# A GRU on one core: five filling units ahead of the first turn of h, none behind the second

## The chip, the cores and the metric

The kernel runs on one NeuronCore of a Trainium2 chip. The metric is the device time of a whole launch in microseconds; the times shown before are three runs of the kernel, and one further execution was profiled.

## The reference

A gated recurrent unit walks over 128 time steps, with 64 batch rows, an input of 512 and a hidden state of 512; its states are added to the input. Everything is float32. Cut to what is computed:

```python
def step(h, inp):
    x_t, prop = inp                      # prop: every fourth step but the last
    comb = jnp.concatenate([x_t, h], axis=-1)
    z = jax.nn.sigmoid(comb @ Wz + bz)
    r = jax.nn.sigmoid(comb @ Wr + br)
    comb2 = jnp.concatenate([x_t, r * h], axis=-1)
    h_cand = jnp.tanh(comb2 @ Wh + bh)
    h_new = (1.0 - z) * h + z * h_cand
    h_next = jnp.where(prop, jnp.tanh(h_new @ Wp + bp), h_new)
    return (h_next, h_new)
out = x + ys                             # ys: h_new of every step
```

Each weight has 1024 rows: the upper 512 act on x_t, the lower 512 on h (or r * h).

## The kernel before

**Layout.** The state of 64 x 512 is held as 128 partitions x 256: the upper 64 partitions have the first half of the hidden units, the lower 64 the second half. A product of the state with 512 x 512 weights needs the state transposed, since the state is the stationary operand of the matmul. `turn` (L195) does this: four bf16 transposes on TensorE move one half of the state (128 columns) into the PSUM tile `turn`, and one copy (L193, by the engine named in the call) brings it into SBUF. The transposed state is `hT`, the transposed r * h is `rhT`; each has two halves, c = 0 and c = 1. `product` (L186) multiplies one quarter of the rows of a weight; a full product of state and weight is four of them, in an order in which the first two need only half c = 0 of the transposed state (16 matmul records in all, 1.91 us).

**A step** (loop over t, 128 times) is written in this order, and each engine runs its instructions in the order of the program (the schedule is written by hand; a framework adds the semaphores):

1. the R product of hT (L576), then `read_out` and, on ScalarE and VectorE, the sigmoid and r * h (L598, L599);
2. the Z product of hT, the turns of r * h into rhT, sigmoids of z (L613, L614) and `keep` = (1 - z) * h (L615); then `fill(places[0])`;
3. the candidate's product of rhT (L624);
4. for each half of 128 columns: tanh on ScalarE (L637), times z on VectorE (L638), plus keep on VectorE (L643), which gives that half of `h_new`;
5. filling units, the turn of the first half of h, copied by VectorE; one unit; the turn of the second half, copied by ScalarE; filling units (L646 to L653);
6. in every fourth step ("prop") a further product with Wp, a tanh and turns of that result;
7. work for later on GpSimd (sums of input products), the addition of h_new to x, DMAs of x in and of results out on SyncE's queue.

The PSUM regions `rc` and `zp` hold the three gates' sums; ScalarE writes the input's part of the next step's gates into them (`seed`, L384), and the recurrent products add to that.

**Filling units.** The products of x with the upper halves of the weights don't depend on h. They are cut into small units that stand in a list (`queue`), and `fill(n)` (L390) puts the next n of them into TensorE's stream at that place. `PLACES` says how many units a step takes in its two or three places:

```python
PLACES = (
    (6, 8, 6), (2, 6), (6, 6), (2, 6), (6, 8, 6), (2, 6), (2, 6), (6, 8),
)
```

The entry is chosen by (t - 3) mod 8. The first number goes ahead of the candidate's product, the second behind it, the third (prop steps) around the turn that follows Wp. From t = 3 on the units are those of `batch` (L427): the inputs of eight steps are multiplied by two levels of a Strassen-like scheme, with 49 products instead of 64; a unit is one such block product, four matmul records of 192 columns, and 14 units make a batch. When the eighth and the fourteenth unit of a batch have been placed, an "end" (copies on ScalarE, additions on VectorE, L450 to L460, which read the PSUM tiles scratch_q, r, a, x) waits in `pending` until the next `read_out`. The first three steps take 12 units in either place, plain products of 256 columns. The units of the last group are used up in t = 122; later steps have none.

Of the kernel before, what the change touches and what calls it, by code (L numbers as in the profile page):

```python
# [17 lines left out]
def kernel(  # L18
# [176 lines left out]
    def turn(src, dst, c, name, eng):  # L195


        pt = turn_ps[c][:, :P].bitcast(BF16).rearrange("p (w n) -> p w n", w=2)
        for s in range(S):
            words = src[:, c * P + s * B : c * P + (s + 1) * B].bitcast(BF16)  # L200
            for w in range(2):
                nc.tensor.transpose(  # L202
                    pt[s * B : (s + 1) * B, w, :],
                    words.rearrange("p (n w) -> p w n", w=2)[:, w, :],
                    ident16,
                )
        copy(
            eng,
            dst[:, c, :].bitcast(U16).rearrange("p (n w) -> p n w", w=2),
            pt.bitcast(U16).rearrange("p w n -> p n w"),  # L210
        )
# [178 lines left out]
    def fill(n):  # L390
        for _ in range(min(n, len(queue))):
            unit, end = queue.pop(0)
            unit()
            if end is not None:
                pending.append(end)

    def read_out():
        while pending:
            pending.pop(0)()
# [157 lines left out]
    for t in range(T):  # L557
# [6 lines left out]
        places = PLACES[u]  # L564
        if t < 3:
            queue.extend(plain(2 * t + 2) + plain(2 * t + 3))
            places = (12, 12)
        elif t == 3:
            queue.extend(batches(FIRST))
            places = (8, 8, 6)  # L570
# [72 lines left out]
            nc.vector.tensor_add(h_new[:, ts(c, P)], pc, keep[:, ts(c, P)])  # L643
        seed(H_, t + 1)
        read_out()
        fill(places[1] - 3 if places[1] > 6 else 4)  # L646
        h = h_new
        if not last:
            hT = new_T("hT", f"hT_{t}")
            turn(h, hT, 0, f"hT_{t}", nc.vector)  # L650
            fill(1)
            turn(h, hT, 1, f"hT_{t}", nc.scalar)
        fill(2 if places[1] > 6 else 1)  # L653
        if t == 2:
            sum_outer_1()
        if t == 3:
# [131 lines left out]
```

## Time and profile before

| what | value |
|---|---|
| median of three runs | 1371.43 us (1371.06 to 1373.5) |
| the profiled execution | 1370.75 us |
| its span, first to last instruction | 1368.9 us |
| mean granted TensorE clock | 0.998 |
| TensorE matmuls, weight loads | 15336 each |
| DMA traffic | 73.86 MB, mean 54 GB/s |

How to read it: PE is TensorE's matmuls, PEld its weight loads, which run ahead of and beside the matmuls; DVE is VectorE, ACT ScalarE, POOL GpSimd, SPq SyncE's queue of DMA issues. A timeline line gives start and duration in us, engine, line of the program, operation, what is written and read, the shape, how many instructions were merged into the line, and in brackets the idle time before it with what ended it. Matmul records overlap each other, as their ends are modelled. `L177` is the line of every matmul of a product or unit, `L202` of every transpose, `L193` of every copy behind a turn; their tiles tell them apart.

### The profile page before, as it was taken

What the parts mean: (1) busy time and instruction counts of PE and PEld (TensorE: products, weight loads), DVE (VectorE), ACT (ScalarE), POOL (GpSimd) and SP (SyncE); (2) the same over time, 40 slices, a digit from 0 to 9 for tenths busy, and PEclk for the clock granted to TensorE, in tenths of its full rate; (3) what the DMA queues carried; (4) which work ended last, traced back from release to release, by engine and by line L of the source; (5) the groups of instructions that cost most, each with busy time, mean ns of one, the idle gap of its engine ahead of it and who ended that gap; (6) DMA issues with size and microseconds to landing.
All of it is one profiled execution on the core that took longest, in us unless ns stands there. A gap on an engine that the chain in (4) does not pass through costs nothing.

```text
span 1368.9 us, 37448 instructions
## 1 busy us (share of the span) xinstructions
PE 1342.6 (98%) x15336; PEld 1028.9 (75%) x15336; DVE 689.2 (50%) x1875; ACT 631.2 (46%) x1857; POOL 938.7 (69%) x1139
## 2 busy tenths in 40 slices
PE   7999999999999999999999999999999999999996
PEld 4777777777777777777777777777777777777764
DVE  4245554555555555554555555555555555555543
ACT  1234445445444445445445444445445445454443
POOL 4327676787767786677686767786677686767740
PEclk9999999999999999999999999999999999999999
DMA  9002212212231222212222131222212222131010
GB/s 286 11 17 48 63 32 63 63 33 63 49 77 32 60 36 63 63 32 63 52 43 63 43 83 34 49 46 63 63 32 63 48 48 63 35 76 33 17 33 16
DMA packets 113572, 73.86 MB, mean 54 GB/s; under 512 B 61556, under 2 KB 109812, under 8 KB 113400
## 3 DMA queue, kind: packets, MB, share of 16 engines
q1 hardware_dynamic: 112336, 69.68, 22.5%
q8 instruction: 121, 1.98, 0.6%
q10 hardware_dynamic: 1064, 1.78, 0.4%
q14 instruction: 51, 0.42, 0.1%
HBM read 39.99 MB, written 16.78 MB: 41 GB/s over the span
## 4 chain that ended last, share of the span: by engine, by line
PE 96%; DMA 2%; DVE 1%; ACT 0%; issue 0%; SPq 0%; DVEq 0%; ACTq 0%
PE rc L177 33%; PE zp L177 20%; PE scratch_q L177 11%; PE scratch_x L177 10%; PE scratch_r L177 10%; PE turn L202 6%; PE scratch_a L177 6%; DMA early<-in_x_dram 1%; DMA wx<-in_L_cond_Wz_dram 1%; DMA wh<-in_L_cond_Wr_dram 1%; DVE h L643 0%; DVE turn L638 0%; ACT xT L193 0%; SPq L93 0%; DVE tw L300 0%
## 5 line engine op out<-in xcount | busy, mean ns | idle before, releaser
L177 PE MATMUL rc<-wh,rhT 128*64 128x256 f32 x2048 | 246.6, 381 | 2.0 <-ACT zp L614 2.0
L485 POOL TENSOR_TENSOR cp<-mb,mb 128x768 f32<-128x768 f32 x75 | 136.6, 1821 | 112.1 <-ACT rc L384 67.1
L177 PEld LDWEIGHTS rc<-wh,rhT 128*64 128x64 f32 x2048 | 158.9, 137 | 55.0 <-ACT zp L614 12.4
L177 PE MATMUL rc<-wh,hT 128*64 128x256 f32 x1536 | 183.1, 380 | 0.5 <-DVE hT L193 0.2
L177 PE MATMUL zp<-wh,hT 128*64 128x256 f32 x1536 | 183.2, 379 | 0.0
L722 POOL TENSOR_TENSOR xr<-xr,h 128x256 f32<-128x256 f32 x127 | 92.5, 729 | 102.1 <-DVE h L643 95.5
L193 DVE COPY rhT<-turn 128x256 uint16<-128x256 uint16 x256 | 96.8, 420 | 127.1 <-PE turn L202 127.1
L638 DVE TENSOR_TENSOR turn<-turn,z 128x128 f32<-128x128 f32 x256 | 75.5, 295 | 161.0 <-ACT turn L637 161.0
L485 POOL TENSOR_TENSOR cp<-mb 128x768 f32<-128x768 f32 x45 | 81.9, 1820 | 108.4 <-ACT rc L384 107.2
L177 PEld LDWEIGHTS zp<-wh,hT 128*64 128x64 f32 x1536 | 117.5, 137 | 47.4
L177 PEld LDWEIGHTS rc<-wh,hT 128*64 128x64 f32 x1536 | 111.6, 137 | 45.2 <-issue 1.0
L598 ACT ACTIVATE turn<-rc 128x128 f32<-128x128 f32 x256 | 55.4, 260 | 156.6 <-issue 85.6
L452 DVE TENSOR_TENSOR cx<-scratch_r,cx 128x384 f32<-128x384 f32 x105 | 58.6, 558 | 128.7 <-ACT cx L450 128.7
L193 ACT COPY hT<-turn 128x256 uint16<-128x256 uint16 x127 | 47.3, 373 | 155.8 <-PE turn L202 96.6
L485 POOL TENSOR_TENSOR mb<-mb,mb 128x768 f32<-128x768 f32 x60 | 109.2, 1820 | 13.4 <-DVE mb L460 13.4
L458 DVE TENSOR_TENSOR mb<-scratch_r,cq 128x384 f32<-128x384 f32 x105 | 58.6, 558 | 88.1 <-ACT cq L457 88.1
L384 ACT COPY rc<-cp 128x256 f32<-128x256 f32 x254 | 95.8, 377 | 11.6 <-POOL s L325 0.4
L637 ACT ACTIVATE turn<-rc 128x128 f32<-128x128 f32 x256 | 57.0, 262 | 90.3 <-PE rc L177 90.3
L613 ACT ACTIVATE z<-zp 128x256 f32<-128x256 f32 x128 | 49.2, 384 | 104.0 <-PE zp L177 104.0
L202 PEld LDWEIGHTS <-h 128*64 128x64 bf16 x1016 | 47.4, 109 | 51.0 <-DVE h L643 46.0
L384 ACT COPY zp<-cp 128x256 f32<-128x256 f32 x127 | 47.9, 377 | 78.1 <-DVE keep L615 78.1
L202 PE MATMUL turn<-ident,h 128*64 128x128 bf16 x1016 | 76.6, 227 | 5.4 <-DVE h L643 5.4
(149 smaller groups left out, 2954.6 us busy)
## 6 DMA issues: line engine op xcount, KB each, us to landing
xr<-in_x_dram SPq DMA_DIRECT2D x62, 256.0 KB, 4.2
out_dram<-xr SPq DMA_DIRECT2D x62, 256.0 KB, 3.3
xs<-in_x_dram SPq DMA_DIRECT2D x56, 256.0 KB, 4.3
wh<-in_L_cond_Wr_dram SPq DMA_DIRECT2D x2, 512.0 KB, 7.6
wh<-in_L_cond_Wz_dram SPq DMA_DIRECT2D x2, 512.0 KB, 8.3
wh<-in_L_cond_Wh_dram SPq DMA_DIRECT2D x2, 512.0 KB, 10.4
early<-in_x_dram SPq DMA_DIRECT2D x4, 256.0 KB, 13.1
wp<-in_L_cond_Wp_dram SPq DMA_DIRECT2D x1, 1024.0 KB
```

The lines of the kernel that those rows point to most:

```text
L177: nc.tensor.matmul(ps[s * B : (s + 1) * B], lhsT=lhs, rhs=rhs(s), start=start, stop=True, skip_group_check=True,)
L193: (eng.copy if eng is nc.scalar else eng.tensor_copy)(dst, src)
L202: nc.tensor.transpose(pt[s * B : (s + 1) * B, w, :], words.rearrange("p (n w) -> p w n", w=2)[:, w, :], ident16,)
L384: nc.scalar.copy(cut(slots[i]), G[t][:, :, i, :])
L452: nc.vector.tensor_add(T2[n], r_ps, T2[n])
L458: nc.vector.tensor_add(blocks()[:, :, 0, 1], r_ps, q2)
L485: nc.gpsimd.tensor_add(dst, a, b)
L598: nc.scalar.activation(act_ps[c], slots[R][:, ts(c, P)], AF.Sigmoid)
L613: nc.scalar.activation(z, slots[Z], AF.Sigmoid)
L637: nc.scalar.activation(pc, slots[H_][:, ts(c, P)], AF.Tanh)
L638: nc.vector.tensor_mul(pc, pc, z[:, ts(c, P)])
L722: nc.gpsimd.tensor_add(xr[g][:, j, :], xr[g][:, j, :], h_new)
```

## The change

Only the second place of a step is cut otherwise. Before: with more than six units, three fewer than all lie ahead of the first turn of h, one between the turns, two behind; with six units four, one and one. After: five ahead, one between, and the rest behind. So steps of eight units keep 5, 1, 2; steps of six go from 4, 1, 1 to 5, 1, 0; the first three steps (twelve units) go from 9, 1, 2 to 5, 1, 6.

```diff
         seed(H_, t + 1)
         read_out()
-        fill(places[1] - 3 if places[1] > 6 else 4)
+        fill(5)
         h = h_new
         if not last:
             hT = new_T("hT", f"hT_{t}")
             turn(h, hT, 0, f"hT_{t}", nc.vector)
             fill(1)
             turn(h, hT, 1, f"hT_{t}", nc.scalar)
-        fill(2 if places[1] > 6 else 1)
+        fill(places[1] - 6)
         if t == 2:
             sum_outer_1()
```

The steps with six units are those whose place in the eight is 1, 2, 3, 5 or 6. The order of instructions on VectorE, ScalarE, GpSimd and SyncE is the same before and after.

## The prediction

> **What bounds the kernel now.** I read the page's busy shares and chain first, then the chain of waits, then the timeline around the end of single steps. The page:
>
> ```profile
> PE 1342.6 (98%) x15336; PEld 1028.9 (75%) x15336; DVE 689.2 (50%) x1875; ACT 631.2 (46%) x1857; POOL 938.7 (69%) x1139
> PE 96%; DMA 2%; DVE 1%; ACT 0%; issue 0%; SPq 0%; DVEq 0%; ACTq 0%
> ```
>
> TensorE is the bound, so the change is worth what it does to TensorE's stream and nothing else. But "98% busy" hides short stalls, because matmul records overlap. The wait list of the weight loads (waited for: us in total, times, longest) shows where the stream is late:
>
> ```profile
> PEld L202 <- DVE h L643: 46.0, 158, 1.6
> ```
>
> The loads of the turns of h (L202) wait for the additions that make h (L643). This is the wait that the fifth unit in front could fill. To see what it costs I took a step of the kind that changes (t=33). Times are us from the span's start:
>
> ```profile
> 401.12 1.95 PE L177 MATMUL rc<-wh,rhT 128*64 128x256 f32 x16
> 403.97 0.29 DVE L643 TENSOR_TENSOR h<-turn,keep 128x128 f32<-128x128 f32 x1
> 404.32 0.15 PEld L202 LDWEIGHTS <-h 128*64 128x64 bf16 x4 [0.30 <-DVE h L643]
> 404.71 0.41 DVE L193 COPY hT<-turn 128x256 uint16<-128x256 uint16 x1
> 404.85 0.15 PEld L202 LDWEIGHTS <-h 128*64 128x64 bf16 x4 [0.24 <-DVE h L643]
> 404.94 0.20 PEld L177 LDWEIGHTS scratch_a<-tw,xT 128*64 128x64 f32 x4
> 405.25 1.52 PEld L177 LDWEIGHTS rc<-wh,hT 128*64 128x64 f32 x16
> 405.32 1.91 PE L177 MATMUL rc<-wh,hT 128*64 128x256 f32 x16
> ```
>
> The candidate's product ends at 401.12 + 1.95 = 403.07; I count from there. First half of h ready at 1.19, first turn at 1.25 (its load waited 0.30), VectorE copies it to hT from 1.64 to 2.05, second turn at 1.78 (waited 0.24), last unit's loads from 1.87, next R product's loads from 2.18. The R loads come 0.13 us after the copy's end: its first operand is just this half of hT. So two things end together here, the last unit and the copy. Which one decides is seen where there are no units at all, at t=124, where the queue is empty:
>
> ```profile
> 1337.73 1.49 PE L177 MATMUL rc<-wh,rhT 128*64 128x256 f32 x12
> 1340.37 0.15 PEld L202 LDWEIGHTS <-h 128*64 128x64 bf16 x4 [1.59 <-DVE h L643]
> 1340.76 0.41 DVE L193 COPY hT<-turn 128x256 uint16<-128x256 uint16 x1
> 1341.29 0.23 PEld L177 LDWEIGHTS rc<-wh,hT 128*64 128x64 f32 x4 [0.25 <-issue]
> ```
>
> Product's end 1339.22; first turn at 1.15, copy from 1.54, R at 2.07. Steps t=5, 13, ... have the same 2.07 with all six units in place. So these steps are bound by a chain (tanh, multiply, add, turn, copy, R), and the six units fit inside it for nothing.
>
> **The change part by part.** No instruction is added or removed; one unit (four matmul records) per step moves from behind the second turn to ahead of the first. Its own cost is unchanged. VectorE, ScalarE, GpSimd and SyncE keep their order; no DMA moves, and no queue other than TensorE's is passed.
>
> *Steps with eight units* (5, 1, 2 before and after) and the prop steps (all have eight): nothing changes.
>
> *The first three steps* (12 units: 9, 1, 2 becomes 5, 1, 6): nothing. Their units are wider, about 0.44 us each (36 records fill the 4.0 us ahead of the turn at t=0), so five cover to about 2.0 us after the product, and h is ready at 1.03 there; six units behind cover the copy. If that cover failed, a turn would wait as at t=124, at most some 0.4 us in each of three steps, 1.2 us.
>
> *The 75 steps with six units* carry the change. The fifth unit ahead fills the wait of the first turn, and the last unit no longer stands between second turn and R. What I need is a step with five units ahead, one between and none behind. The trace has one: at t=122 (a step of eight units) the queue held only six, so its last fill found nothing:
>
> ```profile
> 1317.74 1.26 PE L177 MATMUL rc<-wh,rhT 128*64 128x256 f32 x10
> 1320.12 0.50 PE L177 MATMUL scratch_r<-tw,s 128*64 128x192 f32 x4
> 1320.29 0.29 PEld L202 LDWEIGHTS <-h 128*64 128x64 bf16 x4
> 1320.51 0.21 PEld L177 LDWEIGHTS scratch_r<-tw,s4r 128*64 128x64 f32 x4
> 1320.78 0.42 DVE L193 COPY hT<-turn 128x256 uint16<-128x256 uint16 x1 [0.16 <-PE turn L202]
> 1321.32 1.52 PEld L177 LDWEIGHTS rc<-wh,hT 128*64 128x64 f32 x16 [0.30 <-issue]
> 1321.35 1.95 PE L177 MATMUL rc<-wh,hT 128*64 128x256 f32 x16 [0.17 <-DVE hT L193]
> ```
>
> Product's end 1319.00; fifth unit's matmuls from 1.12, the first turn's load no longer waits but its matmuls follow the fifth unit at 1.45, copy from 1.78 to 2.20, R's loads at 2.32, and R itself is listed as waiting for hT. The stall has not gone; it has moved from the turns of h to the head of R, and is longer, as the fifth unit delays the first turn's matmuls (1.45 against 1.25 at t=33 and 1.14 at t=5), so the copy starts later and nothing covers it.
>
> When R's loads start after the product's end, by step within the eight (averages over all such steps of the timeline):
>
> | steps | count | half h ready | R now | R at t=122's order | loss, summed |
> |---|---|---|---|---|---|
> | t=4, 12, ... | 15 | 1.13 | 2.11 | 2.32 | 3.2 |
> | t=5, 13, ... | 15 | 1.09 | 2.07 | 2.32 | 3.7 |
> | t=6, 14, ... | 15 | 1.21 | 2.19 | 2.32 | 2.0 |
> | t=8, 16, ... | 15 | 1.20 | 2.18 | 2.32 | 2.2 |
> | t=9, 17, ... | 15 | 1.20 | 2.18 | 2.32 | 2.2 |
>
> (t=6, 120 and 121 run as the second row and are summed so.) At worst h is ready at 1.22, its turn could load at 1.27, and the fifth unit lets it load at 1.29: no stall is left ahead, so 2.32 holds for all. Sum 13.3 us by R's loads. By R's first matmul instead (0.07 after its load now, 0.03 at t=122) the same sum is 10.1 us.
>
> Which counts? The Trainium skill, "TensorE: Matmul & The Clock Gate", section "Step-by-step: what each phase is for", says that TensorE's window pulls weight loads ahead of running matmuls while matmuls stay in program order; then a load's start is only a lead, the first matmul is the start, and the loss is 10.1 us. The row says that the lead has shrunk to nothing here and loads pace: R's last matmul ends 1.98 us after its first load in both (405.32 + 1.91 - 405.25; 1321.35 + 1.95 - 1321.32), and the following Z product starts 1.79 and 1.78 us after it. So I count by loads, less 0.01 us for each of 75 steps: 13.3 - 0.8 = **12.5 us**.
>
> A second rule speaks for a gain. "Perfetto Trace Analysis", section "Identifying Performance Opportunities", under "Optimization Strategy", has one find the gaps on the contended engine, see what blocks it, and make that start sooner. The gaps are the 46.0 us above; some 38 us of them lie in the 75 steps (four steps without units at the end have the other 8), so closing them would promise up to 38 us, near 1333. The rows say that this wait is the weight loader's lost lead, not matmul time, and that what follows it, the copy into hT, is not made earlier: +12.5 us.
>
> What is late next: R's first load blocks all behind it on TensorE, so Z, the turn of r*h and the next candidate move with it; the DVE and ACT work that they release moves too. From R's loads to the next candidate's last matmul is 6.00 us at t=122, 124 and the mean of t=5, 13, ... alike, so nothing downstream absorbs it. ScalarE's copy of hT's second half ends 1321.59 at t=122, before R needs it in its second half (eight loads of 0.095 us after 1321.32: 1322.08): no further wait.
>
> Sum against the profiled execution: 1370.75 (span 1368.9 and 1.85 around it) + 12.5 = 1383.3. The median of the runs shown is 0.7 above the profiled execution; between the two I put **1383.6 us**, 0.9% more than 1371.43.
>
> **The rivals.**
> - *Half of it.* In t=6, 8, 9, ... the load of the first turn waits 0.30 us, nearly one unit's loads (0.33), so the fifth unit fits into the wait and only the first two rows lose: 3.2 + 3.7 = 6.9 us, 1378.5. For it: the 0.30. Against: VectorE's copy follows the turn's matmuls, and those move from 1.25 to 1.45.
> - *Faster.* If R could follow the second turn at once: at t=122 that turn starts at 1320.89 and its four transposes take 0.11, so R would start at 2.00, against a mean of 2.21 now: 75 x 0.21 = 16 us less, 1355.5. It decides only if hT's first half has landed by 2.00; at t=122 it lands at 2.20, at t=124 (no unit at all) at 1.95 with R still at 2.07. The saving there would be 0.04 at most.
> - *No change.* The later R is absorbed before the next candidate, 1371. Against: the 6.00 us above.
> - *Worse.* The moved unit meets a scratch bank not yet read out, or the hT copy is queued behind other work; each 0.05 us more in 75 steps is 3.8 us, 1387. The unit moves by at most 0.4 us, and the bank it writes was read out over 1.5 us before (nearest in t=37: L452 ends 445.20, the unit would start about 446.9).
>
> **How the numbers follow.** The forecast 0.80, half 0.08, no change 0.04, faster 0.04, worse 0.04. The forecast's own range is 1381 to 1386 (10.1 to 13.3 us on either baseline, and a little). The wide range takes in the half case at its low end and the worse one at its high end: 1378 to 1388. Within 0.2% (2.7 us) is what a measurement can't tell from no change: faster 0.04, same 0.04, slower 0.92.
>
> **What would show it.** Right: the weight loads' wait for h (46.0 us) falls to a few us; a new wait of R (rc, L177) for VectorE's hT copy appears in some 75 steps; R's loads lie 2.32 us after the candidate's end in all of them; the steps t=12 to 13 take 9.9 instead of 9.72 us; steps with eight units stay. Wrong: R's loads before 2.2, or a step's later part shorter than 6.00 us in the two-unit steps.

## The result and the profile after

The changed kernel takes 1384.46 us (1383.99 to 1385.13, five runs), against 1371.43 before: a ratio of 1.0093, 95% interval 1.0080 to 1.0106. It is 13.0 us slower. The forecast was 1383.6, 0.9% slower.

The profiled execution after took 1384.46 us with a span of 1382.7, 13.8 more than before. Step by step (from the last matmul of one candidate's product to that of the next) the two traces differ by 13.0 us in sum. The other 0.8 lies ahead of these steps: the last matmul of the first candidate's product starts at 39.8 against 39.1 us, before the first place that the change touches. Of the 13.0 us, 13.1 lie in the 75 steps with six units; all other steps differ by under 0.01 us each.

The waits of TensorE's matmuls and of its weight loads after the change (who, for whom: us in total, times, longest):

```profile
PE rc L177 <- DVE hT L193: 12.8, 76, 0.2
PE turn L202 <- DVE h L643: 5.4, 8, 1.1
```

```profile
PEld rc L177 <- issue: 24.2, 82, 0.3
PEld L202 <- DVE h L643: 7.9, 8, 1.6
```

The loads' wait for h has fallen from 46.0 to 7.9 us, and what is left of it belongs to the four last steps that have no units. In its place R's matmuls wait for VectorE's copy into hT, 76 times (75 steps and t=122), for 12.8 us. R's loads wait too: their row has 24.2 us in 82 waits, against 1.0 us in 4 before, but names no releaser ("issue"); the last experiment shows why. The matmuls' own wait for h, as listed, is 5.4 us in 8 waits, as before. (Such a list shows idle time between records, and matmul records overlap; from start to start a smaller part of the 38 us that went from the loads' row had delayed matmuls, see below.) This is how such a move shows in a profile: the wait that was aimed at is gone, and the time is longer.

The timeline of t=33 after the change, the step shown before:

```profile
406.45 0.81 PE L177 MATMUL rc<-wh,rhT 128*64 128x256 f32 x5
408.16 0.29 DVE L643 TENSOR_TENSOR h<-turn,keep 128x128 f32<-128x128 f32 x1
408.36 0.53 PE L177 MATMUL scratch_a<-tw,o 128*64 128x192 f32 x4
408.52 0.31 PEld L202 LDWEIGHTS <-h 128*64 128x64 bf16 x4
408.69 0.31 PE L202 MATMUL turn<-ident,h 128*64 128x128 bf16 x4
409.03 0.42 DVE L193 COPY hT<-turn 128x256 uint16<-128x256 uint16 x1
409.57 1.52 PEld L177 LDWEIGHTS rc<-wh,hT 128*64 128x64 f32 x16 [0.30 <-issue]
409.60 1.95 PE L177 MATMUL rc<-wh,hT 128*64 128x256 f32 x16 [0.17 <-DVE hT L193]
```

From the candidate's end (406.45 + 0.81 = 407.26): h ready at 1.19 as before, the fifth unit's matmuls from 1.10, the first turn's at 1.43 (before 1.25), copy from 1.77 to 2.19 (before 1.64 to 2.05), R's loads at 2.31 (before 2.18). In both kernels they come 0.12 us after the copy's end, in all 75 steps. The mean over every kind of six-unit step is 2.31, as at t=122.

### The profile page after: what moved, and what is told of

It reads as the page before. It is cut to its first block, busy times and chain, and to the rows that moved or that the text cites. A ratio compares the mean times of both kernels' runs of the same rounds, so it can differ in the third digit from the quotient of the medians.

```text
span 1382.7 us, 37463 instructions
## 1 busy us (share of the span) xinstructions
PE 1343.6 (97%) x15336; PEld 1125.6 (81%) x15336; DVE 696.7 (50%) x1875; ACT 628.9 (45%) x1857; POOL 938.0 (68%) x1139
## 4 chain that ended last, share of the span: by engine, by line
PE 94%; DVE 4%; issue 1%; ACT 0%; DMA 0%; ACTq 0%; DVEq 0%
PE rc L177 34%; PE zp L177 20%; PE scratch_q L177 11%; PE scratch_r L177 10%; PE scratch_x L177 10%; PE scratch_a L177 5%; PE turn L202 4%; DVE hT L193 2%; DVE tw L301 0%; DVE tw L300 0%; DVE h L643 0%; DVE turn L638 0%; ACT xT L193 0%; PE rc L160 0%; PE zp L160 0%
## 5 line engine op out<-in xcount | busy, mean ns | idle before, releaser
L177 PEld LDWEIGHTS rc<-wh,rhT 128*64 128x64 f32 x2048 | 168.0, 137 | 46.6 <-ACT zp L614 12.3
L177 PE MATMUL rc<-wh,hT 128*64 128x256 f32 x1536 | 186.6, 383 | 13.2 <-DVE hT L193 12.8
L177 PEld LDWEIGHTS rc<-wh,hT 128*64 128x64 f32 x1536 | 122.9, 136 | 48.6 <-issue 23.6
L177 PEld LDWEIGHTS zp<-wh,hT 128*64 128x64 f32 x1536 | 132.1, 137 | 32.9
L485 POOL TENSOR_TENSOR mb<-mb,mb 128x768 f32<-128x768 f32 x60 | 109.2, 1821 | 13.4 <-DVE mb L460 13.4
L202 PEld LDWEIGHTS <-h 128*64 128x64 bf16 x1016 | 70.0, 110 | 14.9 <-DVE h L643 7.9
## 6 DMA issues: line engine op xcount, KB each, us to landing
early<-in_x_dram SPq DMA_DIRECT2D x4, 256.0 KB, 13.3
```

The source lines that it names most:

```text
L177: nc.tensor.matmul(ps[s * B : (s + 1) * B], lhsT=lhs, rhs=rhs(s), start=start, stop=True, skip_group_check=True,)
L202: nc.tensor.transpose(pt[s * B : (s + 1) * B, w, :], words.rearrange("p (n w) -> p w n", w=2)[:, w, :], ident16,)
L485: nc.gpsimd.tensor_add(dst, a, b)
```

## The experiments

Theory A is that of the prediction: the first turn's matmuls set the time of the copy into hT, the copy sets R, and the fifth unit pushes the turn back. All edits below start from the kernel before and leave the first three steps at 9, 1, 2 and the steps of eight at 5, 1, 2, unless said. "Loads" are R's, counted from the end of the candidate's product.

### A unit behind, or a unit fewer ahead?

The change does two things, a fifth unit ahead and none behind. Two runs do one each. The edit, with the numbers of the first run (the second has 4, 2, 0, the third 3, 1, 2):

```diff
-        fill(places[1] - 3 if places[1] > 6 else 4)
+        six = places[1] == 6
+        fill(5 if six else places[1] - 3)
...
-            fill(1)
+            fill(0 if six else 1)
...
-        fill(2 if places[1] > 6 else 1)
+        fill(1 if six else 2)
```

> Six-unit steps placed 5, 0, 1 (the change's fifth unit ahead, but a unit still behind the second turn). Theory A (the first turn's matmuls, pushed back behind the fifth unit, set the time of the copy into hT and so of R): R's loads 2.32 us after the candidate's end as in the changed kernel, time 1384, 0.9% over before. Rival B (the loss comes from taking away the unit behind the second turn, which covered the copy): 1371, as before, R's loads at 2.07 to 2.19.

Measured: 1383.85 us, ratio 1.0086 (1.0070 to 1.0103). Its t=33, with the product's end at 406.72 + 1.49 = 408.21:

```profile
406.72 1.49 PE L177 MATMUL rc<-wh,rhT 128*64 128x256 f32 x12
409.64 0.66 PE L202 MATMUL turn<-ident,h 128*64 128x128 bf16 x8
409.98 0.42 DVE L193 COPY hT<-turn 128x256 uint16<-128x256 uint16 x1
410.07 0.20 PEld L177 LDWEIGHTS scratch_a<-tw,xT 128*64 128x64 f32 x4
410.52 0.44 PEld L177 LDWEIGHTS rc<-wh,hT 128*64 128x64 f32 x6 [0.26 <-issue]
```

A unit stands behind the second turn again (loads from 410.07), and R's loads come at 2.31 all the same, with TensorE idle ahead of them. The unit behind gives nothing back.

> Six-unit steps placed 4, 2, 0 (nothing behind the second turn, but the first turn where it was before). Theory A: the copy starts as before, and the second turn comes at 1.81 to 1.93 after the candidate's end, R after its transposes; R's loads at 2.07 to 2.19, time 1371 within 3 us. Rival B: the copy stands uncovered, a loss like that of the changed kernel, 1384.

Measured: 1371.54 us, ratio 0.9997 (0.9988 to 1.0005). Nothing stands behind the second turn here, and nothing is lost:

```profile
402.82 1.50 PE L177 MATMUL rc<-wh,rhT 128*64 128x256 f32 x12
405.57 0.31 PE L202 MATMUL turn<-ident,h 128*64 128x128 bf16 x4
405.96 0.41 DVE L193 COPY hT<-turn 128x256 uint16<-128x256 uint16 x1
406.36 0.28 PE L202 MATMUL turn<-ident,h 128*64 128x128 bf16 x4
406.49 0.62 PEld L177 LDWEIGHTS rc<-wh,hT 128*64 128x64 f32 x7
```

Product's end 404.32: turn at 1.25, copy from 1.64, loads at 2.17, as before the change. The two runs together: the whole loss is the fifth unit ahead; the empty place behind costs nothing. Rival B falls.

> Six-unit steps placed 3, 1, 2 (one unit fewer ahead, one more behind). Theory A: the turns can't come earlier, h isn't ready; TensorE stands still for one unit more ahead of the first turn, and then has a unit more to do behind the second: R's first matmul 0.33 us later, 75 x 0.33 = 25 us, 1396. Rival B (more cover behind is better): not slower than 1371. A small loss (under 8 us) would say that TensorE had slack there that the timeline doesn't show.

Measured: 1395.92 us, ratio 1.0176 (1.0161 to 1.0191), 24 us over before and as expected; R's first matmul comes 0.31 to 0.33 us later. The wait of the turns' loads for h rises to 70.2 us and the matmuls now wait too:

```profile
PE turn L202 <- DVE h L643: 23.1, 83, 1.1
```

Before the change the same row of the matmuls was 5.4 us in 8 waits. With three units ahead TensorE does run dry; with four it just about doesn't (its loads lose their lead, its matmuls start about 0.1 us late at each turn); with five it is late. Of the three numbers tried, four is the best, and both neighbours lose.

### Does h hold the first turn?

ScalarE joins two pieces of xT (`join_x`, L263, 0.7 us each) ahead of the tanh in four of the eight steps, and h is 0.04 to 0.12 us later there. The edit puts the second piece behind the second turn; the first run has the order 5, 1, 0, the second 4, 1, 1:

```diff
-        if pair >= 0:
-            for n in range(2):
-                ... join_x(..., n)
+        joins(0)          # the same, for n = 0
...
             turn(h, hT, 1, f"hT_{t}", nc.scalar)
         fill(...)
+        joins(1)          # for n = 1
```

> The changed kernel's order (5, 1, 0), but in the steps in which ScalarE joins two pieces of xT ahead of the tanh (L263, 0.7 us each) the second join stands behind the second turn, so that h is ready some 0.1 us earlier there. Theory A (the fifth unit, not h, holds the first turn): no gain, 1384. Rival C (the chain from tanh on holds R also in the changed kernel): 42 steps x 0.11 = 5 us less, 1379.

> The order of before (4, 1, 1) with the second join moved behind the second turn. Theory A: here h does hold the first turn (its load waits 0.30 us in those steps), so R's loads come at 2.07 us after the candidate's end instead of 2.11 to 2.19: 14 x 0.04 + 42 x 0.115 = 5 us less, 1366.5. Rival C expects the same here; the two runs together tell A and C apart. If the moved join delays ScalarE's later work, less.

Measured: 1384.25 us, ratio 1.0096 (1.0077 to 1.0114), and 1365.95 us, ratio 0.9957 (0.9941 to 0.9973). With five units ahead an earlier h is worth nothing: R's loads stay at 2.31 in every six-unit step. With four it is worth 6 us: loads at 1.99 in t=12, 20, ... and 2.06 in the others. So the fifth unit holds the first turn in the changed kernel, and h holds it before. The gain was 1 us larger than expected, since in t=12, 20, ... R's loads came 0.12 us earlier and not 0.04.

### Is the copy the last link?

The engines of the two copies are exchanged, in the changed order and in that of before:

```diff
-            turn(h, hT, 0, f"hT_{t}", nc.vector)
+            turn(h, hT, 0, f"hT_{t}", nc.scalar)
...
-            turn(h, hT, 1, f"hT_{t}", nc.scalar)
+            turn(h, hT, 1, f"hT_{t}", nc.vector)
```

> The changed kernel's order in the six-unit steps (5, 1, 0), but ScalarE copies the first half of hT and VectorE the second (in every step). Theory A: the copy of the first half is the last link ahead of R; ScalarE's takes 0.37 us instead of VectorE's 0.42, so R's loads come at 2.27 instead of 2.32 and 75 x 0.05 = 4 us return: 1380.5. Rival (R is held by TensorE's own order or by the second half): 1384 or more.

Measured: 1370.99 us, ratio 0.9995 (0.9987 to 1.0004). The direction was right and the size was three times too small: this undoes the whole loss. The timeline of its t=33:

```profile
406.22 0.31 PE L202 MATMUL turn<-ident,h 128*64 128x128 bf16 x4
406.56 0.37 ACT L193 COPY hT<-turn 128x256 uint16<-128x256 uint16 x1 [0.74 <-PE turn L202]
406.99 1.49 PEld L177 LDWEIGHTS rc<-wh,hT 128*64 128x64 f32 x16 [0.18 <-ACT hT L193]
406.99 1.95 PE L177 MATMUL rc<-wh,hT 128*64 128x256 f32 x16
```

The turn and the copy start as in the changed kernel, the copy takes 0.37 instead of 0.42, and R's loads come 0.05 us after its end instead of 0.12, the first matmul with the load. In all six-unit steps the loads lie at 2.20 or 2.21 instead of 2.31. The expectation had the faster copy alone (0.05 us); the load's shorter delay behind it (0.06) and a first matmul that starts with its load and not after it (0.03) come on top. These steps are 10.5 us of the 13.4 by which the steps of the two profiled executions differ. Another 2.9 us lie in the 14 steps t=11, 19, ... (0.21 us each), where the wait of scratch_q's loads for L460, 7.8 us in 15 waits before, is down to one wait of 2.1 us at the start; t=3 takes 0.4 us longer. The likely reason, not tried alone: ScalarE does the hT copy earlier and so is earlier free for the copies behind it.

> The order of before (4, 1, 1) with ScalarE copying the first half of hT and VectorE the second. Theory A: the copy lands 0.1 us earlier, but R's first matmul is then held by the unit behind the second turn (turn at 2.05 plus 0.47), where it already starts now; nothing is gained in the six-unit steps, and only the wait of scratch_q for L460 in the prop steps gets shorter as in the swapped run of the changed order (2.5 us): 1369. If the copy were all that held R before the change: 75 x 0.1 more, 1362.

Measured: 1368.68 us, ratio 0.9978 (0.9969 to 0.9987). As expected: the six-unit steps are unchanged in sum (0.3 us; R's first matmul is where it was, now behind the unit, though its loads come 0.08 us earlier), and 2.5 us come from the prop steps. So with the faster copy the order 4, 1, 1 is still 2.3 us ahead of 5, 1, 0. Before the change copy and last unit ended together; taking away the one leaves the other.

### Both sides shortened

Since copy and units end together, a gain needs both: the copy earlier (ScalarE, h earlier) and no unit held behind the second turn's wait (4, 2, 0).

> Six-unit steps 4, 2, 0, first half of hT copied by ScalarE, second join behind the second turn. Theory A: first turn as early as h allows (1.14 after the candidate's end), copy landed by about 1.87, and TensorE's own work (two units, second turn) holds R's loads to about 2.03: 9 us less in the six-unit steps and 2.5 in the prop steps, 1360. If R can't start before about 2.07 for another reason: 1364.

Measured: 1355.01 us, ratio 0.9879 (0.9863 to 0.9894), 5 us better than expected. R's loads come at 1.99 after the product's end, not 2.03, and at 1.92 in t=12, 20, ...; the six-unit steps gave 13.1 us instead of 9. An earlier h alone moves both the copy and the second turn, and had given 6.7 us in these steps (in the order 4, 1, 1); the swap with 4, 2, 0 but without the earlier h was not run.

The load that needs an engine's copy had shown two delays so far: 0.12 us after VectorE's copy, 0.05 after ScalarE's. In the program R's first matmul waits for VectorE (hT) and for ScalarE; with ScalarE copying, for ScalarE alone. The turns of h wait for VectorE alone, and their loads come 0.05 us after the addition. The candidate's product waits for both (rhT by VectorE), and comes 0.12 us after the copy in all 63 steps in which it waits. That suggests two engines' semaphores (the counters by which one engine tells another that it is done), not VectorE, as the cause. The last run turns this off at the candidate:

```diff
         for c in range(C):
-            turn(rh, rhT, c, f"rhT_{t}", nc.vector)
+            turn(rh, rhT, c, f"rhT_{t}", (nc.scalar, nc.vector)[c])
```

> As the fastest run so far (4, 2, 0, first half of hT by ScalarE, second join moved), and also the first half of rhT copied by ScalarE. In the runs so far the load that needs a VectorE copy (hT or rhT) and also something of ScalarE started 0.11 to 0.12 us after the copy's end, and the load that needs ScalarE alone 0.05 after it. Theory D (waiting for two engines costs about 0.06 us more): the candidate's loads now come 0.05 us after ScalarE's copy in the steps with two units ahead of the candidate; with the copy's 0.37 for 0.42 TensorE is no longer late there, some 0.07 us in 60 steps, 4 us: 1351. Rival E (the 0.11 belongs to VectorE's copies, or ScalarE's sigmoids of z, now behind the copy, come late): the gap stays at 0.11, or the z sigmoids delay keep and h, and the time is 1353 or more.

Measured: 1351.78 us, ratio 0.9851 (0.9835 to 0.9868): 1.5% faster than the kernel before, the fastest here. Its copy and loads (t=33):

```profile
397.92 0.37 ACT L193 COPY rhT<-turn 128x256 uint16<-128x256 uint16 x1 [0.88 <-PE turn L202]
398.34 1.56 PEld L177 LDWEIGHTS rc<-wh,rhT 128*64 128x64 f32 x16
398.47 1.90 PE L177 MATMUL rc<-wh,rhT 128*64 128x256 f32 x16
```

The copy ends at 398.29 and the loads start at 398.34, 0.05 later, in the same 63 steps. The candidate's last matmul follows R's first by 5.85 instead of 5.92 in the steps with two units ahead of it.

Exchanging the engine changes two things at once, who copies and how many engines are waited for. The traces tell them apart. The second wait is an instruction of its own in TensorE's queue, which the timeline leaves out; this is the one ahead of R's loads at t=33 after the change (duration in ns, then the start):

```profile
L177 PEldq EVENT_SEMAPHORE  x1: 51/51/51, 409.5 to 409.5; - x1
```

It waits for VectorE's semaphore and starts 0.04 us after the copy's end, takes 0.05, and the load, which itself waits for ScalarE's, starts 0.025 later: 0.12 in sum. (That is also why the list of waits names no releaser for the load.) It stands there in all 75 six-unit steps before and after the change and in none of the runs with the swap; ahead of the candidate's loads it stands in 64 steps of every run but the last, and there in none. So Theory D holds in both places where it was switched, and Rival E falls: the semaphore instruction starts as soon behind VectorE's copy (0.04 us) as a load behind ScalarE's (0.05), and what is added is the instruction between.

## Why the prediction was right

*The analogue.* The prediction took t=122, where the queue happened to run out after 5 and 1 units (a piece of luck for the forecaster), as the picture of all 75 changed steps: R's loads at 2.32. Measured 2.31 in each of the five kinds of step. That the loss is smaller where h was late came out too: t=5 to 6 grew by 0.25 us, t=8 to 9 by 0.14.

*Which start counts.* The two counts of the loss were 10.1 us (first matmuls) and 13.3 us (loads). The time from R's loads to the start of the next candidate's last matmul is the same before and after in all five kinds (5.99 us with two units ahead of the candidate, 7.23 with six), so the loads count. The prediction's correction of 0.01 us a step, 0.8 in sum, did not show: 13.1 us in the six-unit steps against its 12.5. This is the only term of the sum that was mis-sized by more than 0.2 us. The Trainium skill ("TensorE: Matmul & The Clock Gate", "Step-by-step: what each phase is for") has TensorE pull weight loads ahead of running matmuls; read so that the first matmul is the start, it gives 10.1 and would have been 3 us short here: a load that waits for data has no lead, and then the chain goes through it. Where R's loads do have a lead the first matmul counts: with the swap in 4, 1, 1 the loads came 0.08 us earlier and the steps did not get shorter.

*The wait that was removed.* 38 us of the turns' waits went away as predicted and brought no time. The prediction called this wait the loads' lost lead and not matmul time; that holds for the larger part of it. From start to start, the first matmul of the two turns came 0.24 and 0.22 us after the matmul ahead of it before the change and 0.13 after it, in all some 15 us in the 75 steps. Some 17 us came back at the head of R, whose first matmul follows at 0.39 us instead of 0.16. "Perfetto Trace Analysis" ("Identifying Performance Opportunities", "Optimization Strategy") has one make that start sooner which blocks the gap. The change didn't do this, it filled the gap with other work; the run that did make h sooner (4, 1, 1 with the second join moved) took this row from 46.0 to 37.2 us and gained 6 us.

*What costs nothing.* The first three steps changed by under 0.01 us and so did the steps with eight units, as said. TensorE's lists show no new wait for GpSimd or a DMA.

*The rivals.* Half the loss (by its own sum 1378.3 us, not 1378.5) would have needed the copy to follow the turn's load; in t=8, 9, 16, 17, ... that load came 0.02 us later, its matmuls 0.18 and the copy 0.14, so it followed the matmuls. The faster rival needed the copy landed by 2.00; it landed at 2.20. The reading that copy and last unit end together was confirmed from both sides: taking away either alone (4, 2, 0, or the swap in 4, 1, 1) moved the six-unit steps by 0.5 us in sum or less, and both together, with h earlier, gave 13.1 us, of which the earlier h alone had given 6.7.

## What to carry to other kernels

Filling work ahead of a dependent step should end just before its input is ready: a unit too many delays the chain by itself even where it fits into a wait of the weight loads, a unit too few leaves the engine dry. To value a wait, follow it to the next instruction that the chain needs (here turn, copy, R) and look in the trace for a step that already has the new order, such as the last ones in which a queue runs out. Where two things end together, shorten both. And where a load starts later behind a copy than its like elsewhere, look for a semaphore instruction in its queue.

## What the runs showed of the hardware

A weight load that waits for one engine started about 0.05 us after that engine's instruction ended (ScalarE's copies of hT and rhT, VectorE's additions of h). One that waits for VectorE and ScalarE started 0.12 us after VectorE's copy, if that came last (hT in the 75 six-unit steps of the changed kernel, rhT in 63): a semaphore instruction of 0.051 us stands ahead of it in TensorE's queue. Moving the copy to the other engine involved, so that one wait is left, was worth 0.06 us in addition to the 0.05 that ScalarE's copy of this shape (0.37 us) is shorter than VectorE's (0.42). A copy by ScalarE with a second wait kept was not tried, so it stays open whether the second wait costs anything where it has ended before.
